# TensorE's order in a two-layer perceiver: weights turned before the next keys, norms between two halves of the values, other pauses and other places for products

## The chip, the cores and the metric

The kernel runs on one core of a Trainium2 chip. The metric is the time of one execution on the device, in microseconds (us). Its engines are TensorE (PE, with its weight loads as PEld), VectorE (DVE), ScalarE (ACT), GpSimd (POOL) and SyncE (SP), which issues most of the transfers. Each works through its own list of instructions in order and waits for the others by semaphores. All arithmetic is in float32.

## The reference, cut to what matters

`x` holds 64 batch rows of 32 tokens of 256 numbers, the context 64 rows of 257. Two layers of three steps each work on `x`; LN is a layernorm without weights.

```
x = x + cross0(ctx, LN(x))   # 16 heads x 64; keys: 257 normed context rows and the 32 queries
x = x + self0(LN(x))         # 16 heads x 16, 32 tokens, rms-normed q and k
x = x + moe(LN(x))           # 64 experts, top 8, 128 places each, and a shared expert
x = x + cross1(LN(x), ctx)   # 16 heads x 64; keys: the 257 raw context rows
x = x + self1(LN(x))         # latent heads of 32 with rotation, causal
x = x + tanh(LN(x) @ W @ A1 @ A2 + bias)
```
In `cross0` the queries and keys of each head are divided by their root mean square before they meet, so the squares of all keys must be summed before a score is complete:
```
q = (ln @ Wq); k, v = split(concat([LNg(ctx), ln]) @ Wkv)     # per head: 64 numbers
sim = (rms(q) * gq / 8) @ (rms(k) * gk).T;  out = softmax(mask(sim)) @ v;  return out @ Wout + bout
```

## The kernel before, in words

**Tiles and blocks.** The 2048 tokens are 16 tiles of 128, that is four batch rows (NB = 4) each. A batch row with its context is a block: 64 blocks s, with tile t = s // 4 and b = s % 4. `Kernel.run` calls three stages one after the other: `before` (first layer's attention and the routing, to 1568 us in the profile), `experts` (to about 1777 us) and `after` (second layer, to the end).

**What sets the order.** TensorE executes its instructions in the order in which the program writes them; the calls in the loops are that order, written by hand. The other engines' instructions are ordered by a scheduler, which also chooses, for `nc.any.tensor_copy`, whether VectorE or ScalarE copies. Products land in eight banks of TensorE's accumulator memory, which all share one rotation (`bank`): a product that needs a bank waits until the one that had it has been read.

Work that belongs to a whole tile is written as generators: `queries` ahead of a tile, `tail` and `follow` behind it. A `yield` is a pause. `slot()` lets every generator that is under way advance by one pause, tails ahead of fronts, so that pieces of a tile's work fall between the pieces of the next tile's blocks. In the first layer a block holds two `slot()` calls, or one in a tile's fourth block, where a new tail is added; in the second layer it holds three.

**First layer, one block** (`CrossFirst`, loop at the end of `before`). `load` brings the context rows (`cx`, 256 KB). `prepare` norms them (L140 on VectorE, L1160 and L1161 on GpSimd). `turn` transposes them on TensorE (L1173), and ScalarE copies them to `xT` (L1176). `keys` makes eight products with the key weights (L167, 128x289); ScalarE and VectorE copy them in turns (L1201, L1203), and ScalarE squares each half once four are there (L1206, `sq`). `norms` sums the squares on TensorE (L1218); VectorE clamps (L1226) and ScalarE takes logarithms (L1227), `nk`. `spread` brings `nk` to all rows on TensorE (L1239), and ScalarE exponentiates (L1240). `scores` are the products of queries and keys (L1258); VectorE multiplies them by the factors (L1267), adds the mask (L1268), and the softmax follows (row maximum L182 on VectorE, exponentials L184 on ScalarE, L187 to L197). `weigh` turns the weights on TensorE (L207) and copies them to `at` (L208). `values` multiplies them by the context (`weighed`, L221, eight products in two halves `kc`, and L231 for the rest of the keys) and copies both halves to `yT` (L233). The loop works on several blocks at once: in turn s it makes keys, norms and scores of block s + 2, weights and values of block s, and turns block s + 3.

**The tail of a tile** in the first layer: `heads_out` (value weights, copies `oT` L253, output weights), a pause, then `self_first`: layernorm `z`, its transposition (L149, copied to `zT` L150), the query, key and value products (`sw`, L535 to L546), transpositions (L552), scores (L573), softmax (`softmax_heads`, L267 to L271), and `attend_self` (VectorE's exponent sums and transposition L295 and L297, L310 on TensorE, `oTs` L319, output weights `swo`). In `attend_self` there is a pause before L310, and a second one only where `self.slack` is set, which is in the second layer. Then `route`: gate product, top 8, places, and the scatter of tokens to the experts' buffer (L645). The tail of the last tile but one (t == nt - 2) pauses HOLD = 5 times more ahead of `self_first`, so that it runs beside the last one's.

**Experts.** A loop over 64 experts, whose weights (L668 and L673) are fetched AHEAD = 12 experts early; pieces of the shared expert lie between them. At e == 12 `after_weights` loads and prepares the second layer's weights. Its last step is `ffn_weights`, which multiplies W, A1 and A2 of the last feed-forward into one matrix (loads `f_*`, products L167 `psA<-f_a,f_a1T` and `psA<-mid,f_wT`).

**Second layer** (`CrossSecond`, loop in `after`). Keys are never formed: `queries` makes `qk` for a tile (the key weights folded into the queries, L1308 to L1326, with the layernorm `z` of that tile ahead). In turn s come the scores of block s + 2 (L167 `psY<-xT,qk`, then maximum L1357 on VectorE, exponentials L1358 on ScalarE, scaling L1363), a `slot()`, `weigh(s)` (L1375, copies L1376), a `slot()`, `values(s)` (L167 `psA<-at,cx`, L1388), a `slot()`. Blocks 0 and 1 have two `slot()` calls more. `follow` is the tail: `heads_out`, then `self_second` (z and zT; the latent product with `wl`, L979, into the tile `lat`; L994, L995 and the rotation L988; its transposition L1003; `qTl` copied by ScalarE, L1005; the product with `wqk` and `qf`, L1011; keys turned, L1014, copied to `kTl`, L1016; scores L1026; exponentials L1036), `attend_self` and `ffn` (L1069 to L1074, and the store of the tile). The tail of the last tile but one pauses HOLD = 5 times more ahead of `self_second`. The tile `lat` has one buffer.

The start of `before` does blocks 0 and 1 in a short loop of its own (load, turn, keys, norms, spread, scores), as there is nothing to lay between.

## Time and profile before

| | |
|---|---|
| three runs | 2803.31, 2801.76 and 2800.55 us, median 2801.76 us |
| the profiled execution | 2804.67 us |
| its span, first to last instruction | 2802.8 us |
| TensorE's mean granted clock, as a share of full speed | 0.982 |
| VectorE, ScalarE, GpSimd busy | 1694.9, 1241.6 and 684.3 us |

By stage, in us (the granted clock is the mean over the stage; "DMA" is the mean busy share of the 16 transfer engines):

| stage | from | to | length | PE busy | DVE busy | ACT busy | clock | DMA |
|---|---|---|---|---|---|---|---|---|
| start, first tile | 0 | 180 | 180.0 | 143.4 | 88.6 | 78.6 | 0.93 | 0.35 |
| first layer's loop | 180 | 1525.75 | 1345.75 | 1317.1 | 859.6 | 736.2 | 1.00 | 0.08 |
| last tails | 1525.75 | 1568.5 | 42.75 | 25.1 | 24.4 | 10.0 | 0.74 | 0.59 |
| experts | 1568.5 | 1770 | 201.5 | 193.1 | 68.2 | 58.8 | 0.97 | 0.72 |
| second layer's loop | 1770 | 2700 | 930.0 | 903.6 | 603.0 | 336.7 | 1.00 | 0.20 |
| last tile and tails | 2700 | 2802.8 | 102.8 | 75.4 | 51.1 | 21.1 | 0.83 | 0.04 |

How to read the profile. A line of waits gives the engine, the tile and the line of the waiting instructions, after the arrow what released them, and then the sum of the waiting time, how often, and the longest. A line of the timeline gives the start in us, the duration of a group, the engine, line and operation, output and inputs with their shapes and the number of instructions; what stands in brackets is the time waited just before, and for whom. The busy digits of the page give tenths in 40 equal slices of the span, some 70 us each. A TensorE that is reported busy may still be slower than it could be, since the ends of its products are modelled: the distance from the start of one group to the start of the next is the surer measure.

### The profile page before, as it was taken

What the parts mean: (1) busy time and instruction counts of PE and PEld (TensorE: products, weight loads), DVE (VectorE), ACT (ScalarE), POOL (GpSimd) and SP (SyncE); (2) the same over time, 40 slices, a digit from 0 to 9 for tenths busy, and PEclk for the clock granted to TensorE, in tenths of its full rate; (3) what the DMA queues carried; (4) which work ended last, traced back from release to release, by engine and by line L of the source; (5) the groups of instructions that cost most, each with busy time, mean ns of one, the idle gap of its engine ahead of it and who ended that gap; (6) DMA issues with size and microseconds to landing.
All of it is one profiled execution on the core that took longest, in us unless ns stands there. A gap on an engine that the chain in (4) does not pass through costs nothing. (4 is left out here: it accounts for less than half of the span.)

```text
span 2802.8 us, 58905 instructions
## 1 busy us (share of the span) xinstructions
PE 2657.6 (95%) x23386; PEld 1824.5 (65%) x23386; DVE 1694.9 (60%) x4427; ACT 1241.6 (44%) x3436; POOL 684.3 (24%) x756
## 2 busy tenths in 40 slices
PE   6999999999999999999999799999999999999996
PEld 3556666666666666666666578667777777777764
DVE  5546666666666666666665433466666666666664
ACT  3455555555555555555554223333333333333331
POOL 5211333133313331243121200321212222121001
PEclk8999999999999999999999899999999999999997
DMA  8000011011000000000001677321211222222110
GB/s 271 16 14 18 31 33 31 18 31 33 29 18 27 26 22 18 20 19 16 18 7 38 233 237 243 91 67 54 58 51 50 59 52 58 56 51 55 33 35 5
DMA packets 136087, 157.03 MB, mean 56 GB/s; under 512 B 24024, under 2 KB 118979, under 8 KB 135812
## 3 DMA queue, kind: packets, MB, share of 16 engines
q1 hardware_dynamic: 114308, 119.65, 13.8%
q0 software_dynamic: 12288, 25.21, 3.4%
q10 hardware_dynamic: 9216, 8.39, 0.9%
q8 instruction: 185, 3.03, 0.4%
q14 instruction: 90, 0.74, 0.1%
HBM read 121.63 MB, written 37.75 MB: 57 GB/s over the span
## 5 line engine op out<-in xcount | busy, mean ns | idle before, releaser
L167 PE MATMUL psA<-xT,wk 128*128 128x289 f32 x2048 | 517.4, 411 | 7.9 <-ACT xT L1176 4.5
L167 PEld LDWEIGHTS psA<-xT,wk 128*128 128x128 f32 x2048 | 388.0, 191 | 134.8 <-issue 21.8
L780 POOL DMA_INDIRECT y<-oute,idx x128 | 131.5, 1028 | 643.4 <-DVE x L791 453.9
L167 PE MATMUL psA<-at,cx 128*128 128x512 f32 x512 | 235.4, 602 | 20.0 <-ACT qTl L1005 18.2
L221 PE MATMUL psY<-at,cx 128*128 128x512 f32 x512 | 239.8, 612 | 0.1
L167 PE MATMUL psY<-xT,qk 128*128 128x257 f32 x1024 | 234.3, 382 | 0.0
L167 PEld LDWEIGHTS psY<-xT,qk 128*128 128x128 f32 x1024 | 190.8, 190 | 35.0 <-issue 10.2
L1357 DVE TENSOR_REDUCE mx<-psY 128x1 f32<-128x257 f32 x256 | 105.7, 423 | 133.6 <-PE psY L167 133.5
L1358 ACT ACTIVATE sim<-psY,mx 128x257 f32<-128x257 f32 x256 | 121.6, 476 | 142.3 <-DVE mx L1357 142.2
L184 ACT ACTIVATE sim<-sim,mx 128x289 f32<-128x289 f32 x256 | 134.1, 526 | 100.0 <-DVE mx L182 100.0
L221 PEld LDWEIGHTS psY<-at,cx 128*128 128x128 f32 x512 | 93.5, 192 | 123.0 <-issue 108.8
L167 PEld LDWEIGHTS psA<-at,cx 128*128 128x128 f32 x512 | 92.9, 190 | 120.8 <-issue 76.7
L233 ACT COPY yT<-psY 128x512 f32<-128x512 f32 x127 | 68.2, 589 | 220.7 <-PE psY L231 220.7
L645 POOL DMA_INDIRECT buf<-z,fi x128 | 126.5, 988 | 148.0 <-DVE fi L642 102.2
L1160 POOL TENSOR_TENSOR cx<-cx,a_gx 128x512 f32<-128x512 f32 x64 | 81.8, 1278 | 292.1 <-DVE cx L140 290.3
L1206 ACT ACTIVATE sq<-kT 128x1156 f32<-128x1156 f32 x128 | 149.4, 1167 | 4.4 <-DVE kT L1203 2.8
L1201 ACT COPY kT<-psA 128x289 f32<-128x289 f32 x256 | 94.8, 389 | 104.2 <-PE psA L167 104.2
L1376 ACT COPY at<-psT 128x512 f32<-128x512 f32 x145 | 78.8, 595 | 123.4 <-PE psT L1375 118.3
L1218 PE MATMUL psB<-sq,c 128*32 128x289 f32 x1024 | 109.4, 419 | 19.7 <-ACT sq L1206 19.5
L1388 DVE SCALAR_TENSOR_TENSOR yT<-at,xT,psA 128x512 f32<-128x512 f32 x128 | 94.0, 735 | 56.1 <-PE psA L167 50.7
L167 PE MATMUL psY<-yT,wv 128*64 128x128 f32 x2048 | 121.6, 275 | 1.6 <-DVE yT L1388 1.4
L1177 POOL COPY xT<-lnT 128x64 f32<-128x64 f32 x64 | 15.3, 240 | 423.0 <-PE psA L167 299.3
(257 smaller groups left out, 5190.5 us busy)
## 6 DMA issues: line engine op xcount, KB each, us to landing
cx<-in_ctx SPq DMA_DIRECT2D x128, 256.0 KB
we<-in_m_ew SPq DMA_DIRECT2D x64, 384.0 KB
xT<-in_ctxT SPq DMA_DIRECT2D x64, 257.0 KB
buf<-zero SPq DMA_DIRECT2D x32, 256.0 KB
be<-buf SPq DMA_DIRECT2D x64, 128.0 KB
oute<-oe ACTq DMA_DIRECT2D x64, 128.0 KB
mu<-in_mask SPq DMA_DIRECT2D x16, 128.5 KB
x<-in_x SPq DMA_DIRECT2D x16, 128.0 KB
```

The lines of the kernel that those rows point to most:

```text
L167: self.nc.tensor.matmul(ps, lhsT=lhs[i], rhs=rhs[i], start=(i == 0), stop=(i == n - 1))
L184: nc.scalar.activation(sim[:, g, :], sim[:, g, :], AF.Exp, bias=mx[:, g : g + 1], accum_out=sm[:, g : g + 1])
L221: nc.tensor.matmul(ps[kc], lhsT=values[i][:, kc * P : (kc + 1) * P], rhs=at[i], start=(i == 0), stop=(i == n - 1 and tail is None),)
L645: d = nc.gpsimd.indirect_dma_start(out=self.buf[:, :], out_offset=bass.IndirectOffsetOnAxis(ap=fi[:, k : k + 1], axis=0), in_=z[:, 0, :], ...
L780: nc.gpsimd.indirect_dma_start(out=y, out_offset=None, in_=self.oute[:, :], in_offset=bass.IndirectOffsetOnAxis(ap=self.idx[:, t, k : k + ...
L1160: nc.gpsimd.tensor_tensor(cx, cx, self.gx.unsqueeze(1).to_broadcast([P, 2, D]), ALU.mult)
L1201: nc.scalar.copy(kT[:, p, :], ps[:, :JK])
L1206: nc.scalar.activation(sq[p // 4], kT[:, p - 3 : p + 1, :], AF.Square)
L1218: nc.tensor.matmul(ps[g * 32 : (g + 1) * 32, :JK], lhsT=k.pair[odd], rhs=sq[p // 4][:, p % 4, :], start=(odd == 0), stop=(odd == 1),)
L1357: nc.vector.tensor_reduce(mx[:, g : g + 1], ps[:, :J], AX.X, ALU.max, negate=True)
L1358: nc.scalar.activation(sim[:, g, :], ps[:, :J], AF.Exp, bias=mx[:, g : g + 1], accum_out=sm[:, g : g + 1])
L1388: nc.vector.scalar_tensor_tensor(self.yT[:, c, :, b * S : (b + 1) * S], self.at[:, 2, :].rearrange("p (h i) -> p h i", h=H), xT[:, c, J - ...
```

## The change

It moves work in TensorE's order and changes one buffer; no product is added or taken away.

- **First layer, a block.** `weigh(s)` stands ahead of `keys(s + 2)` now, not behind it. `weighed` does one half per call, and `norms(s + 2)` stands between the halves; both halves are copied to `yT` after the second.
- **`attend_self`** always has the second pause ahead of L310; before, only in the second layer.
- **The start.** The blocks 0 and 1 are written out: loads 2 to 4 come first, and `turn(1)` and `turn(2)` stand ahead of the norms of the block before.
- **HOLD** is 8 pauses in the first layer and 9 in the second, where both were 5.
- **`ffn_weights`** is called at expert 24, and no longer at expert 12 at the end of `after_weights`.
- **Second layer.** `scores(s + 2)` stands behind `weigh(s)`, between the first and the second `slot()` of a turn, where it stood ahead of both. `lat` has the two buffers of its pool.

```diff
@@ -30,7 +30,7 @@
 CAP = 128
 GT = 4
 AHEAD = 12
-HOLD = 5
+HOLD = 8, 9
 TOPK = 8
 FI = 128
 FS = 512
@@ -209,30 +209,27 @@
             k0 += n
         return [at[:n, j, :] for j, n in enumerate(sizes)]
 
-    def weighed(self, yT, b, at, values, tail=None):
+    def weighed(self, yT, b, kc, at, values, tail):
+
 
 
 
         nc = self.nc
-        ps = [self.bank("psY") for _ in range(2)]
-        n = len(at)
-        for kc in range(2):
-            for i in range(n):
-                nc.tensor.matmul(
-                    ps[kc],
-                    lhsT=values[i][:, kc * P : (kc + 1) * P],
-                    rhs=at[i],
-                    start=(i == 0),
-                    stop=(i == n - 1 and tail is None),
+        if kc == 0:
+            self.psy = [self.bank("psY") for _ in range(2)]
+        ps = self.psy
+        for i in range(len(at)):
+            nc.tensor.matmul(
+                ps[kc], lhsT=values[i][:, kc * P : (kc + 1) * P], rhs=at[i], start=(i == 0), stop=False
+            )
+        if kc == 1:
+            for c in range(2):
+                r = slice(64 * c, 64 * c + 64)
+                nc.tensor.matmul(ps[c], lhsT=tail[1][r, :], rhs=tail[0][r, :], start=False, stop=True)
+            for c in range(2):
+                nc.any.tensor_copy(
+                    yT[:, c, :, b * S : (b + 1) * S], ps[c].rearrange("p (h i) -> p h i", h=H)
                 )
-        if tail is not None:
-            for kc in range(2):
-                r = slice(64 * kc, 64 * kc + 64)
-                nc.tensor.matmul(ps[kc], lhsT=tail[1][r, :], rhs=tail[0][r, :], start=False, stop=True)
-        for kc in range(2):
-            nc.any.tensor_copy(
-                yT[:, kc, :, b * S : (b + 1) * S], ps[kc].rearrange("p (h i) -> p h i", h=H)
-            )
 
     def heads_out(self, t, yT, wv, wo, bias, split=False):
 
@@ -296,8 +293,7 @@
         eT = self.wk.tile([P, H, S], F32, name="eT", bufs=self.eb)
         nc.vector.transpose(eT.rearrange("p a b -> p (a b)"), e.rearrange("p a b -> p (a b)"))
         yield
-        if self.slack:
-            yield
+        yield
 
 
         ps = [self.bank("psY") for _ in range(NB)]
@@ -420,18 +416,22 @@
         next(first)
         next(first)
         cross.prepare(1)
-        for i in range(2):
-            cross.load(i + 2)
-            cross.turn(i)
-            cross.keys(i)
-            cross.norms(i)
-            done(first)
-            cross.spread(i)
-            cross.scores(i)
-        cross.load(4)
+        for i in range(2, 5):
+            cross.load(i)
+        cross.turn(0)
+        cross.keys(0)
+        done(first)
+        cross.turn(1)
+        cross.norms(0)
         cross.prepare(2)
+        cross.spread(0)
+        cross.scores(0)
+        cross.keys(1)
+        cross.turn(2)
+        cross.norms(1)
         cross.prepare(3)
-        cross.turn(2)
+        cross.spread(1)
+        cross.scores(1)
 
         wv = self.load(w, "wv", [P, 2, HD], a["a_wv"].rearrange("(k p) n -> p k n", p=P))
         wo = self.load(w, "wo", [P, 8, D], a["a_wo"].rearrange("(k p) n -> p k n", p=P))
@@ -488,13 +488,15 @@
                 fronts.append(cross.queries(t + 1))
             if s + 5 < n:
                 cross.load(s + 5)
+
+            cross.weigh(s)
             if s + 2 < n:
                 cross.keys(s + 2)
-            cross.weigh(s)
             slot()
+            cross.values(s, 0)
             if s + 2 < n:
                 cross.norms(s + 2)
-            cross.values(s)
+            cross.values(s, 1)
             if s + 2 < n:
                 cross.spread(s + 2)
             slot()
@@ -519,7 +521,7 @@
         yield
         if t == self.nt - 2:
 
-            for _ in range(HOLD):
+            for _ in range(HOLD[0]):
                 yield
         yield from self.self_first(t, sw, swo, sg)
         yield from self.route(t, gw)
@@ -759,6 +761,8 @@
             outer(e)
             if e == AHEAD:
                 self.after_weights()
+            if e == 2 * AHEAD:
+                self.ffnw = self.ffn_weights(self.w2)
         done(side)
 
         side, sums = shared(nt // GT - 1), self.combine(0)
@@ -803,7 +807,6 @@
         bo = self.row(w, "bo", a["b_bo"], D)
         self.weights = wq, wkT, wv, wo, bo
         self.lat = self.latent_weights(w)
-        self.ffnw = self.ffn_weights(w)
 
     def after(self, ctx):
         self.eb = self.vb = 1
@@ -838,14 +841,14 @@
             t, b = divmod(s, NB)
             if s + 3 < n:
                 cross.load(s + 3)
-            if s + 2 < n:
-                cross.scores(s + 2)
             if b == NB - 2 and t + 2 < self.nt:
                 steps.append(cross.queries(t + 2))
                 if t + 3 < self.nt:
                     steps.append(self.combine(t + 3, 3))
             slot()
             cross.weigh(s)
+            if s + 2 < n:
+                cross.scores(s + 2)
             slot()
             if s < 2:
 
@@ -863,7 +866,7 @@
         yield from self.heads_out(t, yT, wv, wo, bo)
         if t == self.nt - 2:
 
-            for _ in range(HOLD):
+            for _ in range(HOLD[1]):
                 yield
         yield from self.self_second(t, *self.lat)
         yield from self.ffn(t, *self.ffnw)
@@ -970,7 +973,7 @@
     def self_second(self, t, wl, bl, wvo, bvo, wqk, bqk, wo, bo):
         nc = self.nc
         _, zT = yield from self.normed(t)
-        lat = self.wk.tile([P, 2 * H, LAT], F32, name="lat", bufs=1)
+        lat = self.wk.tile([P, 2 * H, LAT], F32, name="lat")
         latf = lat.rearrange("p h l -> p (h l)")
         for n in range(2):
             ps = self.bank("psA")
@@ -1275,12 +1278,12 @@
         at = k.keyed(sim, [P, P, P])
         self.weights = at[:2], [cx[:, 0, :], cx[:, 1, :]], (at[2], c3)
 
-    def values(self, s):
+    def values(self, s, kc):
         k = self.k
         b = s % NB
-        if b == 0:
+        if b == 0 and kc == 0:
             self.yT = k.wkx.tile([P, 2, H, P], F32, name="yT", bufs=1)
-        k.weighed(self.yT, b, *self.weights)
+        k.weighed(self.yT, b, kc, *self.weights)
 
 
 class CrossSecond:
```

## The prediction

> **What bounds the kernel now.** I read the page's first two parts, then TensorE's waits, its timeline in each stage, and VectorE's and ScalarE's timelines beside it. The profiled execution took 2804.67 us, its span is 2802.8 and the median of the runs shown is 2801.76; the sum below is made against the profiled one, and 2.9 us come off at the end for the median.
>
> ```profile
> PE 2657.6 (95%) x23386; PEld 1824.5 (65%) x23386; DVE 1694.9 (60%) x4427; ACT 1241.6 (44%) x3436; POOL 684.3 (24%) x756
> PE   6999999999999999999999799999999999999996
> PEclk8999999999999999999999899999999999999997
> ```
> TensorE is the bound: 95% busy at a mean granted clock of 0.982. The change takes no product away, so all it can win is the 145 us of gaps, the half speed that follows them, and waits that the modelled busy time hides. TensorE's waits say where the gaps are:
>
> ```profile
> PE psB L1218 <- ACT sq L1206: 19.5, 23, 2.1
> PE psA L167 <- ACT qTl L1005: 18.2, 12, 1.7
> ...
> PE psY L310 <- DVE at L208: 14.7, 14, 1.3
> ...
> PE psA L167 <- DMA f_a<-in_f_a: 4.8, 1, 4.8
> PE psA L167 <- ACT xT L1176: 4.5, 5, 1.8
> ```
> The hidden part is read from start to start in the timeline. The norms of the keys (L1218) need 1.11 us when nothing is late (356.22 to 357.33). In the third block of a tile:
>
> ```profile
> 402.28 1.47 PE L207 MATMUL psT<-c,sim 128*128 128x128 f32 x12
> 403.59 0.60 PE L552 MATMUL psT<-c,qk 128*128 128x128 f32 x4
> 404.12 0.68 PE L1218 MATMUL psB<-sq,c 128*32 128x289 f32 x4
> 405.50 1.17 PE L1218 MATMUL psB<-sq,c 128*32 128x289 f32 x12 [0.70 <-ACT sq L1206]
> 406.60 3.70 PE L221 MATMUL psY<-at,cx 128*128 128x512 f32 x8
> ```
> From 404.12 to 406.60 is 2.48: 1.37 too much, of which the waits name 0.70. By the same reading a tile of 93.5 us loses 0.67 in its second block's norms, 1.37 in the third's, in the fourth 1.24 before L310 and 0.67 in the norms, and 0.47 at L573: 4.4 us.
>
> **1. The first layer's loop, order of a block.** After the scores come now: turned weights (L207, 1.31), keys (7.85), first half of the values (1.82), norms. Nothing is added to TensorE. What decides is how long after the scores' end the second square (L1206) is ready: VectorE's sums and row maxima, four exponentials on ScalarE, the copies of the keys. From the timelines that is about 14.0 us in the second block (scores end 649.25, square 663.26), 11.9 in the third (674.15, 686.06), 12.4 in the fourth (695.58, 707.99). The new order needs it in the third block at 0.93 (turning the queries) + 1.31 + 7.85 + 0.53 + 1.82 + 0.14 = 12.6: the 1.37 go. In the second, with 3.5 of query products and 0.8 of the tail's steps between, at about 16: the 0.67 go. In the fourth at 1.31 + 7.85 + 1.82 + 0.14 = 11.1, so 1.3 of wait stay; that block wins only 0.2, since its chain, not TensorE, sets its length. The first block wins nothing. L310 comes one pause later, behind the spreading; there it meets the wait of L573, which is 0.47. Sum 2.0 a tile, times 14 tiles with a tail beside them: **-28**. The built order puts 331 of the 384 copies `at` on ScalarE (198 now), three of 0.58 us ahead of the exponentials, while ScalarE waits for VectorE's maximum anyway (1.93 idle at 702.12): cost nothing, and up to 1.7 a block without that cover. The norms' path to the spreading (clamp 0.45, Ln 0.45, some 1.3 to 2.2 in all) keeps 3.0 of cover, from 4.8. Turning the weights needs a softmax that ended some 10 us earlier. Ends: 0 if the chain grows by 1 us; -49 if all waits but 2 x 0.47 go (3.5 x 14).
>
> **2. The start.** The first tile's blocks have no tail beside them. Keys begin at 88.91, 109.56, 134.13 and 156.66; a block without waits is 17.3 (7.91 + 1.40 + 1.11 + 3.63 + 1.06 + 0.70 + 0.53 + 1.13, with 0.93 for queries in the first), so 2.4 + 7.3 + 5.2 = 14.9 are lost. xT's copy is now covered by the weights; 1.2 of square wait a block stay: -11, and -1 for the prologue, where the norms of block 1 still wait for the same chain: **-12** (-4 to -16). Two loads `cx` (256 KB each) move ahead on SP's queue, behind the key weights, which they leave alone; the value weights behind them are first needed near 166.
>
> Here the clock matters. The windows 124 to 128 and 148 to 152 had 0.67 and 0.68 granted, after waits of 1.98 + 0.80 and 2.10.
>
> The Trainium skill ("TensorE: Matmul & The Clock Gate", "Why this matters for your kernels") has the clock fall only after gaps over about 3 us; by it these short waits would cost their length alone and the 7.3 would be some 1.5 less. The rows above show the fall after shorter gaps, so the rows count.
>
> **3. Feed-forward products at expert 24.**
> ```profile
> 1633.27 3.75 PE L167 MATMUL psA<-f_a,f_a1T 128*128 128x256 f32 x8 [4.80 <-DMA f_a<-in_f_a]
> 1636.82 2.86 PE L167 MATMUL psA<-mid,f_wT 128*128 128x256 f32 x8
> ```
> Loads issued at 1628.50 to 1629.45, because their space was the latent weights', are used at once. After a 4.80 gap the two products take 3.55 and 2.70 from start to start, 1.76 each at full clock (16 such in 3.51). In the new order SP issues them behind the same point, and TensorE has twelve experts and four shared products (about 25 us) before it needs them: 4.8 + 1.8 + 0.9 = **-7.5** (0 if they were late again). The 768 KB stand ahead of expert weights that have twelve experts of lead: nothing.
>
> **4. The second layer's start.** Scores of block 2 now stand behind the turned weights of block 0, and those behind z of tile 1.
> ```profile
> 1785.67 10.69 PE L167 MATMUL psY<-xT,qk 128*128 128x257 f32 x48
> 1800.46 0.69 PE L149 MATMUL psT<-c,z 128*128 128x128 f32 x2 [4.10 <-DVE z L140]
> ```
> The last third of the 10.69 (3.6) loses its place beside VectorE's chain. That chain loses four maxima and some 0.4 apiece, so z comes about 1.7 earlier: **+2** (0 to +5).
>
> **5. The second layer's loop.** Scores move between the turned weights and the values:
> ```profile
> 2068.21 1.47 PE L1375 MATMUL psT<-c,sim 128*128 128x128 f32 x12
> 2071.18 3.67 PE L167 MATMUL psA<-at,cx 128*128 128x512 f32 x8 [1.50 <-ACT qTl L1005]
> 2074.69 1.02 PE L167 MATMUL psB<-qTl,wqk 128*128 128x512 f32 x2
> 2075.55 0.60 PE L1014 MATMUL psT<-c,lat 128*128 128x128 f32 x4
> 2075.99 0.38 PE L149 MATMUL psT<-c,z 128*128 128x128 f32 x2
> 2076.20 3.64 PE L167 MATMUL psY<-xT,qk 128*128 128x257 f32 x16
> 2079.78 1.29 PE L1026 MATMUL psB<-kTl,qf 32*32 32x32 f32 x128
> ```
> The 1.5 a tile goes: -18.2. But the same 3.64 lay ahead of L1026, between two pauses that now follow each other. kTl's copy (0.58, some 0.8 with its signals) has only a transposition of 0.22 over it: 0.55 a tile. The same happens to zT ahead of the latent product: uncovered it costs 0.46 in the last tile (2757.62). 14 x 1.0 = +14, so **-4** (-14 if covered, +4 if z of the feed-forward, with 0.4 of slack, is late too).
>
> **6. Longer pauses.** The tail of tile 14 now runs three steps ahead of the last tile's, not six or seven. Before the experts, about 4 us of its products (z, 2.75 of sw, L552) leave the stretch ahead of 1525.75 and fill gaps behind it, where TensorE is busy 25.0 of 42.7; but VectorE's two softmax chains (6.15 from L573 to L310) then run side by side, and a step in front delays the last tile's: my walk gives +3 to the chain, 1 for two lost covers: **0** (-5 to +5). At the end, z, wl and wvo of tile 14 (5.0) move behind 2744.16, but stand between wv and wo of the last tile, 4.6 on its chain, and the second softmax adds 1 to 2: **+1** (-4 to +6). The second buffer for lat costs nothing.
>
> **Sum.** -28 - 12 - 7.5 + 2 - 4 + 0 + 1 = -48.5: 2756 for the profiled execution, **2753 us** for the median.
>
> **Rivals.**
> *The square stays late.* ScalarE's copies `at` lengthen the chain by about 1 us, 1 and 2 win nothing but 8 at the start: 2801.8 - 8 - 7.5 + 2 - 4 + 1 = 2785. For it: the fourth block is bound by that chain already. Against: ScalarE idles before the exponentials.
> *Slower.* The three copies (1.7 us) fall behind the exponentials and lengthen the chain by x: the loop then pays x in the fourth block, x - 0.7 in the third, x - 0.9 in the second. The others' 20.5 and the 28 are used up at x = 1.7 (3x - 1.6 = 3.5 a tile); at 2.2 it is 14 x 1.5 = 21 more: about 2823. Against it: in the built order the copies stand ahead of the exponentials in three blocks of four.
> *More than forecast.* The chain shortens by the `at` copies VectorE loses (0.64 each), and the fourth block's wait goes too: 1.3 x 14 = 18 more, 2735.
> *The pauses do not do what they say*: the last tails are chains of VectorE, and 6 is 0; that is in the forecast.
>
> **How the numbers follow.** Forecast 0.58, square late 0.22, more 0.14, slower 0.06. The range 2728 to 2790 takes in the first three with their ends. About 0.2% (5.6 us) can be told from no change: faster 0.91, same 0.04, slower 0.05.
>
> **What would show it.** Right: no wait of L1218 in blocks two and three, one near 1.3 in the fourth; L310's 14.7 down to some 3; no wait for f_a and 1.8 us products; qTl's 18.2 gone, with new rows for kTl near 0.5 and zT near 0.4, fourteen each; a gap near 6 before z at the second layer's start. Wrong: ScalarE's square further than 13 us from the scores' end; spreading waiting for nk; scores waiting for a bank.

## The result: slower, by as much as the forecast was faster

| | median of the runs | profiled execution | its span | granted clock |
|---|---|---|---|---|
| before | 2801.16 us | 2804.67 | 2802.8 | 0.982 |
| after | 2853.2 us | 2851.57 | 2849.7 | 0.974 |

The ratio is 1.0179, with a 95% interval of 1.0163 to 1.0195. The forecast was 2753 with a range of 2728 to 2790. The page of after:

```profile
PE 2665.8 (94%) x23386; PEld 1829.0 (64%) x23386; DVE 1658.1 (58%) x4306; ACT 1305.5 (46%) x3557; POOL 703.0 (25%) x756
PE   6999999999999999999999799899999999999995
PEclk9999999999999999999999899999999999999996
```
No product was added, and TensorE's busy time grew by 8 us where the span grew by 47. TensorE's longest waits in after, as total, count and longest:

```profile
PE psR L1242 <- ACT nk L1230: 37.9, 15, 2.8
PE psT L149 <- DVE z L140: 28.0, 9, 6.4
PE psB L1221 <- ACT sq L1209: 18.6, 19, 2.3
PE psB L1029 <- DVE qf L1014: 18.2, 13, 3.8
```
(Lines move by two to four in after: L1242 is the spreading, L1239 before; L1229 the clamp, L1226 before; L1221 the norms, L1218 before; L306 is L310 and L1029 is L1026.) The waits of L310 for the copies `at`, of the second layer for qTl, and for f_a are gone, as forecast. In their place the spreading waits for nk, which waited 1.7 us in all before.

Where the time went is seen best if the span is cut at products that have the same work ahead of them in either order: the scores of the third tile's first block, those of the last tile's, the second layer's first products of the values (psA<-at,cx), and those of its tile 14.

| stretch | before | after | change | best version (run 15) |
|---|---|---|---|---|
| start and two tiles | 226.56 | 214.65 | -11.9 | 211.63 |
| first layer, 13 tiles | 1216.56 | 1258.55 | **+42.0** | 1169.85 |
| last tile, experts, second layer's start | 367.24 | 368.46 | +1.2 | 357.52 |
| second layer, 14 tiles | 851.95 | 854.76 | +2.8 | 851.61 |
| last two tiles and tails | 140.52 | 153.31 | **+12.8** | 140.14 |

The expectations below cut the last stretch at the turned weights of tile 14, 143.85 before and 160.11 after. That mark flatters the old order: there 16 products of the scores (3.64 us) stand ahead of it, in the new one behind it, so 3.6 of those 16.3 are no loss.

A tile of the first layer went from 93.5 to 96.8 us in the mean (94.5 to 98.9). From keys to keys, its four blocks took 20.5, 21.6, 29.6 and 21.9 before, and in the mean 19.2, 21.0, 30.1 and 26.5 after. The fourth loses 4.6 and the third 0.5; the other two gain. (Blocks are counted here by the keys that are made, the first being those of b = 0. The prediction counts by the turn, two blocks behind: its third, fourth, first and second block are the first to fourth here.) TensorE's timeline of one such fourth block in after:

```profile
655.41 7.97 PE L167 MATMUL psA<-xT,wk 128*128 128x289 f32 x32
663.22 0.33 PE L167 MATMUL psA<-sel,c 128*128 128x64 f32 x2
663.39 0.39 PE L167 MATMUL psA<-count,c 128*128 128x64 f32 x2
...
665.65 1.21 PE L1221 MATMUL psB<-sq,c 128*32 128x289 f32 x16
666.79 1.99 PE L222 MATMUL psY<-at,cx 128*128 128x512 f32 x4
668.71 1.13 PE L228 MATMUL psY<-at,c 64*128 64x512 f32 x4
672.61 1.34 PE L1242 MATMUL psR<-nk,c 32*128 32x289 f32 x8 [2.77 <-ACT nk L1230]
673.88 3.92 PE L167 MATMUL psA<-sw,zT 128*128 128x512 f32 x8
```
The two `sel` and `count` lines are the tail's products for the places of its tokens. They stand behind the keys now. Before, one pause earlier, they stood ahead of them:

```profile
742.78 0.43 PE L167 MATMUL psA<-sel,c 128*128 128x64 f32 x2
743.05 0.39 PE L167 MATMUL psA<-count,c 128*128 128x64 f32 x2
...
746.76 7.97 PE L167 MATMUL psA<-xT,wk 128*128 128x289 f32 x32
...
756.19 1.85 PE L1218 MATMUL psB<-sq,c 128*32 128x289 f32 x16
```
In after the norms follow, the second half of the values, and a hole of 2.77 us. The eight products of sw behind it take 3.92 where they take 2.85 in before: for 3.41 us from 672.67 the granted clock was 0.50. VectorE's timeline in the same stretch of after tells why nk is late:

```profile
664.29 2.58 DVE L140 TENSOR_SCALAR cx<-cx,mv,rs 128x256 f32<-128x256 f32 x2
667.39 0.97 DVE L631 TENSOR_TENSOR val<-val,kept 128x64 f32<-128x64 f32 x1
668.65 1.04 DVE L636 SCALAR_TENSOR_TENSOR junk<-val,v,pr 128x64 f32<-128x64 f32 x1
...
671.41 0.28 DVE L636 SCALAR_TENSOR_TENSOR junk<-val,v,pr 128x64 f32<-128x64 f32 x1
...
671.62 0.46 DVE L1229 TENSOR_SCALAR nk<-psB 128x289 f32<-128x289 f32 x1
```
The norms ended at 666.86; the clamp began 4.76 later, after seven of the eight accumulations (L636) and what belongs to them. In before it began 0.22 after the norms (758.04 to 758.26), with this chain already done, by 753.66:

```profile
753.36 0.28 DVE L634 SCALAR_TENSOR_TENSOR junk<-val,v,pr 128x64 f32<-128x64 f32 x1
...
758.26 0.45 DVE L1226 TENSOR_SCALAR nk<-psB 128x289 f32<-128x289 f32 x1
```
So the theory to test was: **the extra pause in `attend_self` moved not only L310 but everything behind it in the tail, and put VectorE's place chain (L627 to L644) ahead of the clamp.** (A first-layer block holds three `slot()` calls, and a tile's fourth turn two, not two and one as said ahead of the prediction: a tile has eleven pauses.) The rival: the new order of a block leaves too little cover between norms and spreading whatever the pauses are.

### The profile page after: what moved, and what is told of

The parts are those of the page before. It is cut to its first block, busy times and chain, and to the rows that moved or that the text cites. A ratio compares the mean times of both kernels' runs of the same rounds, so it can differ in the third digit from the quotient of the medians.

```text
span 2849.7 us, 58999 instructions
## 1 busy us (share of the span) xinstructions
PE 2665.8 (94%) x23386; PEld 1829.0 (64%) x23386; DVE 1658.1 (58%) x4306; ACT 1305.5 (46%) x3557; POOL 703.0 (25%) x756
## 3 DMA queue, kind: packets, MB, share of 16 engines
q8 instruction: 185, 3.03, 0.4%
## 5 line engine op out<-in xcount | busy, mean ns | idle before, releaser
L222 PE MATMUL psY<-at,cx 128*128 128x512 f32 x512 | 248.6, 609 | 0.0
L222 PEld LDWEIGHTS psY<-at,cx 128*128 128x128 f32 x512 | 88.6, 190 | 95.6 <-issue 92.9
L647 POOL DMA_INDIRECT buf<-z,fi x128 | 128.6, 1005 | 55.2 <-issue 36.1
L1206 DVE COPY kT<-psA 128x289 f32<-128x289 f32 x256 | 109.5, 450 | 17.3 <-PE psA L167 16.5
L167 PEld LDWEIGHTS psY<-yT,wv 128*64 128x64 f32 x2048 | 113.2, 137 | 9.7 <-issue 4.8
L1180 POOL COPY xT<-lnT 128x64 f32<-128x64 f32 x64 | 21.3, 332 | 394.1 <-PE psA L167 280.9
L167 PE MATMUL psY<-wo,oT 128*128 128x256 f32 x512 | 117.6, 383 | 0.0
L1270 DVE TENSOR_TENSOR sim<-psB,sim 128x289 f32<-128x289 f32 x256 | 101.3, 448 | 27.7 <-PE psB L1261 27.6
```

What stands on the lines that cost most here:

```text
L167: self.nc.tensor.matmul(ps, lhsT=lhs[i], rhs=rhs[i], start=(i == 0), stop=(i == n - 1))
L222: nc.tensor.matmul(ps[kc], lhsT=values[i][:, kc * P : (kc + 1) * P], rhs=at[i], start=(i == 0), stop=False)
L647: d = nc.gpsimd.indirect_dma_start(out=self.buf[:, :], out_offset=bass.IndirectOffsetOnAxis(ap=fi[:, k : k + 1], axis=0), in_=z[:, 0, :], ...
L1206: nc.vector.tensor_copy(kT[:, p, :], ps[:, :JK])
L1270: nc.vector.tensor_tensor(sim[:, g, :], ps[i][:, :JK], sim[:, g, :], ALU.mult)
```

## The experiments

Runs 1 to 4, 5 to 8, 9 to 12 and 13 to 15 were each on one chip, and not on the same. On two of these, and on the result's, before takes 2801 to 2802 us; on two (runs 1 to 8) it takes 2821. So a run is compared with before on its own chip, and stretches between chips of one kind. Runs 4 to 6, 9, 10, 13 and 14 are single executions.

**1. One pause ahead of L306 in the first layer.**
```diff
-        yield
+        if self.slack:
+            yield
```


> The changed kernel with one pause ahead of L306 in the first layer again (the second only in the second layer). Theory A, place chain: the extra pause puts the 17 VectorE instructions of a tile's places (L627 to L644) ahead of the clamp of the fourth block's norms (L1229), so the spreading (L1242) waits 2.8 us and TensorE runs 1.1 to 2.5 us slower behind it. Without the pause they stand ahead of the keys' copies, as before: the waits of L1242 for nk (37.9 us) go, the fourth block falls from 26.1 to 27.5 down to 22 or less, a tile takes 91 to 93 us (now 96.2 to 97.6; 93.5 before), and the kernel about 2853 - 14 x 4.6 = 2789 us (2780 to 2800). Theory B, cover: the new order of a block leaves half of the values as cover between the norms and the spreading, which is too little with or without the pause: L1242 still waits over 25 us in all, a tile stays above 95 us, the kernel above 2835 us.

Measured: 2789.15 us on a chip where before takes 2820.61, ratio 0.9886 (0.9869 to 0.9902). The 13 tiles took 1198.2 us, 87.5 less than in the next run, which has both pauses on the same chip. Theory B, above 2835, is out. That the expected 2789 was met is luck: it was counted down from 2853, and on a chip of this kind after takes 2894 (run 6), so the pause cost more here. Not as expected: L1242 still waited 20.6 us in all; see "a second kind of chip" below. Run 12 shows that wait gone on the first kind.

**2. HOLD at 5 and 5.**
```diff
-HOLD = 8, 9
+HOLD = 5, 5
```


> The changed kernel with HOLD at 5 pauses in both layers again. Theory A: the last 160.1 us (from the start of tile 14's blocks in the second layer; 143.9 before) are long because the tails of tiles 14 and 15 run as chains side by side behind the last block, each step of the one in front of the other; with 5 pauses they fall back to about 145 us, and the end of the first layer (372.8 us between the last tile's first keys and the second layer's first turned weights) changes by less than 3: about 2853 - 15 = 2838 us. Theory B: the stretch is long because the scores now stand behind the turned weights; then it stays at about 160 us and the kernel at 2853.

The last stretch took 147.15 us, not 160.1 (140.3, not 153.3, by the table's mark): theory A. The total, 2882.42 (ratio 1.0215, 1.0198 to 1.0232), was not the 2838 expected, since this chip loses more in the loop (1285.7 us against 1258.6 for the same code).

**3. Pause behind the norms.**
```diff
-            slot()
             cross.values(s, 0)
             if s + 2 < n:
                 cross.norms(s + 2)
+            slot()
             cross.values(s, 1)
```


> The changed kernel with the pause between keys and values moved behind the norms: first half of the values, norms, pause, second half. Both pauses ahead of L306 stay. Theory A, place chain: the places' VectorE work now stands behind the clamp in program order, so the wait of L1242 goes with the extra pause in place: a tile at 91 to 94 us, the kernel at 2785 to 2805. The square may be waited for a little more, 1 to 2 us a tile, since the pause's products no longer lie ahead of the norms. Theory B, cover: the wait of L1242 stays, a tile above 95, the kernel above 2835.

The clamp followed the norms' end by 0.05 us in all 14 tiles and the wait for nk was gone: so far theory A. But the kernel took 2892.61 us (1.024, 1.022 to 1.0259), a miss for both. In its place TensorE waits at L1138 and L207 for nothing that the profile names, 17.8 and 17.7 us in all; in run 2, on the same chip and with the pause where it was, these were 14.4 and 3.4. What the edit does on a chip of the first kind was not run. TensorE's timeline behind the fourth block's scores:

```profile
684.24 0.33 PE L1138 MATMUL psT<-c,q 128*128 128x128 f32 x1
685.32 0.60 PE L1138 MATMUL psT<-c,q 128*128 128x128 f32 x4 [0.75 <-issue]
686.78 0.53 PE L1138 MATMUL psT<-c,q 128*128 128x128 f32 x3 [0.86 <-issue]
```

**4. The pause alone, added to before.** (The diff of run 1 reversed, on before.)


> The kernel before with nothing changed but the second pause ahead of L310. Theory A: the wait of L310 for VectorE's copies (14.7 us) goes, and the place chain now stands ahead of the clamp here too; but all eight products of the values and the rest (4.8 us) lie between norms and spreading, and only the 8 or 9 first of the chain stand ahead of the clamp, so at most 1 us of wait a tile comes: 2787 to 2805 us. Theory B (the pause is harmless): 2787 us and no wait of L1239 for nk.

2946.23 us where before takes 2820.61: a large miss, in the direction of the theory, though not by the clamp: it is 3.9 behind the norms in the fourth block, but no spreading waits there. The pause is worse still in the old order: a tile's second block takes 24.2 us (21.6) and its fourth 28.6 (21.9 to 23.4 in before on such a chip), and the norms wait for the square 53 times (53.7 us). I had looked at the clamp alone, though the pause moves oTs, z, gate and places, each into another block's chain.

**5 and 6. Before and after again, on one chip.**


> The kernel before, unchanged, with a trace from the chip of this call. Theory A (chips differ): in the runs so far the kernel before took 2801 us on one chip and 2821 on another. If this call's chip is like the first, the trace is that of before: a tile of 93.5 us, the clamp of the fourth block's norms 0.2 us behind the norms' end, the total near 2801. If it is like the second, 1.4 us a tile are lost while GpSimd issues the scatter (L645), in TensorE's issue or in the clamp, and the total is near 2821: 14 x 1.4 = 20. Theory B (the loss came from the changed order alone): tiles of 93.5 us on any chip, and the 20 us lie elsewhere.

> The changed kernel, unchanged, on the chip of this call. On a chip like the first: tiles of 96.2 to 97.6 us and about 2853 us. On one like the second: tiles of 98 to 99 us, as in the run with HOLD 5, and some 13 us more at the end than that run: 2880 to 2895 us. In both the clamp of the fourth block starts 4.7 us behind the norms' end, since that is the places' chain on VectorE.

2821.64 and 2894.32 us, the second kind of chip. The last stretch was 143.8 and 159.9 (140.4 and 153.0 by the table's mark): the end's loss is the same on both kinds. The loop was 1228.6 and 1295.5.

**7. One pause, HOLD 8 and 5.**
```diff
-HOLD = 8, 9
+HOLD = 8, 5
```


> The changed kernel with one pause ahead of L306 in the first layer, and HOLD at 8 in the first and 5 in the second layer. Theory A: the two losses add up, so against the run with one pause alone it wins the end's 13 us: the stretch from tile 14's first turned weights in the second layer to the end is about 147 us, not 160, and the ratio to before about 0.9886 - 13/2820 = 0.984. Theory B (the end is long because of the scores' new place): the stretch stays at 160 and the ratio at 0.9886.

2778.56 us, ratio 0.9848 (0.9832 to 0.9864), the last stretch 147.3 (140.5 by the table's mark): theory A, within 0.001.

**8. And the second layer's scores back ahead of the pause.**
```diff
+            if s + 2 < n:
+                cross.scores(s + 2)
             if b == NB - 2 and t + 2 < self.nt:
...
             cross.weigh(s)
-            if s + 2 < n:
-                cross.scores(s + 2)
```


> The kernel of the run before this one, with the second layer's scores back ahead of the pause, where the kernel before has them. Theory A: the scores' new place trades one wait for another, since 1.5 us for qTl in each tile became 1.2 us for qf, and in some tiles 1 to 2 us more at a lower clock; with the old place the second layer's regular stretch of 14 tiles takes 858.0 us as before, 2 less than after, and its last stretch 143.9, 3 less than with the scores moved: 3 to 6 us faster than the run before. Theory B, as forecast (-4 for the move): 4 us slower.

2770.89 us, ratio 0.9826 (0.981 to 0.9842), 7.7 less than run 7. The second layer's 14 tiles took 851.6 (857.9 in run 7): theory A, and more than its 3 to 6. The last stretch went from 147.3 to 143.3 by the expectation's mark, but from 140.5 to 140.0 by the table's, so the scores' place costs the end 0.5. HOLD 9 is the rest of the end's +12.8: 12.6 from run 6 to 7, 9.9 from run 1 to 2 (both pairs also differ in the first layer).

**9 and 10. After and before without GpSimd's scatter.** (The eight `indirect_dma_start` of L647 taken out.)


> The changed kernel without GpSimd's scatter (L647, eight a tile): the tokens are not brought to the experts, which work on the cleared buffer; all else stays. Theory A (two separate losses): the place chain on VectorE is still there, so the clamp of the fourth block starts 3.5 to 4.7 us behind the norms' end and L1242 still waits in each tile; but what the second and third chip lost on top (tiles of 98 to 99 us where the first had 96.2 to 97.6) goes, on any chip: tiles of 95.5 to 97.5 us, no issue waits at L1138, about 2840 to 2855 us in all. Theory B (the scatter itself is what moved into the way): the clamp starts within 1 us of the norms' end, tiles fall below 93 us, the kernel below 2810.

> The kernel before without GpSimd's scatter (L645), the same part left out as in the run before this one. Theory A: on the second and third chip TensorE's completions were seen by the other engines only when the scatter had landed (the clamp 3.6 to 5.1 us behind the norms' end, 0.2 on the first). Without a scatter the clamp follows within 0.3 us on any chip, the tile takes 93.5 us or a little less, and the kernel 2795 to 2803 us where before takes 2821 on the same chip. Theory B (another cause on those chips): the clamp stays late and the kernel at 2821.

2843.51 and 2801.79 us; before took 2801.53 on this chip. After's loop was 1254.8 (1258.6 with the scatter): its loss is there without any scatter, as theory A has it. Of the second kind of chip these two runs say nothing, since theirs is of the first.

**11. The fourth block's pause ahead of the spreading.**
```diff
+            if b == 1:
+                slot()
             if s + 2 < n:
                 cross.spread(s + 2)
-            slot()
+            if b != 1:
+                slot()
```


> The kernel of the run with one pause, HOLD 8 and 5 and the scores back (2770.9 us, 0.9826 of before, on the third chip), with the second pause of a tile's fourth block moved ahead of the spreading: 2.85 us of the tail's products (sw) then lie between norms and spreading, beside the half of the values. Theory A (the spreading waits for nk 1.5 to 2.1 us because the clamp is held while the scatter lands): the wait of L1243 (21.6 us in all) goes, the fourth block takes 21.9 us in every tile, 15 to 22 us less on a chip like the second and third (ratio 0.975 to 0.978), 0 to 5 less on one like the first. Rival: the factors of the scores come 2.85 us later and the softmax with them, so the next block's square is waited for instead: no gain.

2751.23 us, 0.9819 (0.9803 to 0.9835), loop 1176.4. Against run 12 on the same chip the fourth block takes 21.70, not 21.22: on this chip, where nk is in time, the edit costs 0.5 a tile. There is no gain, as the rival has it, but not for its reason: the wait for the square is 7.6 us in all in both runs. What it would do on the second kind stays open.

**12. What is left: order of a block, start, lat.**
```diff
-HOLD = 8, 9
+HOLD = 5, 5
...
         self.lat = self.latent_weights(w)
+        self.ffnw = self.ffn_weights(w)
...
-            if e == 2 * AHEAD:
-                self.ffnw = self.ffn_weights(self.w2)
```
together with the diffs of runs 1 and 8.


> The changed kernel with one pause, HOLD 5 and 5, the scores back and the feed-forward products back at expert 12: what is left of the change is the order of a block in the first layer, the start, and the second buffer of lat. Against the run with HOLD 8 and 5 and the scores back (0.9826 of before): the feed-forward products wait for f_a again and run at half clock, 3.3 to 5 us in the experts' stretch (about 208 us from the first shared product to the last expert, 203 with the later place), and the last tails before the experts change by under 5 us. Together 3 to 9 us slower: ratio 0.984 to 0.986.

2741.61 us, ratio 0.9788 (0.9772 to 0.9804): better than expected. The loop took 1169.9 us, a tile 89.98, with 19.2, 19.9, 29.7 and 21.2 in its blocks, and TensorE's waits in 13 tiles add up to 2.5 us, all of them at L573 (0.2 a tile). The clamp stands 0.07 us behind the norms, and the spreading waits for nothing. The experts' stretch was 208.1, as expected with the products early. From the last turned weights of the first layer to the first shared product it took 52.4; run 11, with HOLD 8, took 58.0. So HOLD 8 costs 5.6, where the pause is single; run 7, which has no moved pause, also took 58.0, on the other kind of chip.

**13. The place chain shortened.**
```diff
-        for k in range(TOPK):
-            nc.vector.scalar_tensor_tensor(
-                junk, val, v8[:, k : k + 1], pr, ALU.is_equal, ALU.mult, accum_out=self.w8[:, t, k : k + 1]
-            )
+        nc.vector.tensor_copy(self.w8[:, t, :], top)
```


> The changed kernel, both pauses and HOLD 8 and 9, without the eight accumulations that bring the routing weights into the order of the places (L636, 8 a tile): the eight best weights are copied as they come, so the experts' outputs are weighted wrongly. Theory A (the length of VectorE's chain): 8 x 0.28 to 0.36 = 2.3 to 2.9 us less stand ahead of the clamp, which starts about 2 us behind the norms' end, not 4.7; the half of the values covers 3.0, so the wait of L1242 falls from 2.8 to under 1 a tile, the clock stays up behind it, a tile takes 91 to 94 us (96.2 to 97.6), and the kernel 2780 to 2805 us where after takes 2853, on a chip like the first. Theory B (GpSimd's arithmetic on cx, or the scatter, holds VectorE anyway): the clamp stays 4 us or more late, tiles above 95.

2811.19 us, just above the expected 2780 to 2805; before took 2801.94. The clamp stood 3.16 behind the norms (I had said 2), and L1242 waited 1.17:

```profile
656.44 1.13 PE L228 MATMUL psY<-at,c 64*128 64x512 f32 x4
658.74 0.77 PE L1238 MATMUL psR<-nk,c 32*128 32x289 f32 x8 [1.17 <-ACT nk L1226]
659.44 2.85 PE L167 MATMUL psA<-sw,zT 128*128 128x512 f32 x8
```
The tile took 93.2 us and the loop 1215.3, 43 less than after. Half of the pause's loss in the loop is thus the length of these accumulations: 1.6 of wait a tile, and the granted clock, which has no low stretch in this loop (sw 2.85 behind 1.17) and twelve in after's.

**14. Before without the scatter, once more.**


> The kernel before without GpSimd's scatter, once more (the tokens are not brought to the experts). On a chip where before takes about 2821 us: theory A (the scatter's landing holds TensorE's completions) 2795 to 2805 us, the clamp within 0.3 us of the norms' end; theory B 2815 to 2825. On a chip where before takes about 2801 us both give 2802, as in the first such run.

2799.74 us, on a chip of the first kind again. Not settled.

**15. Run 12 with the feed-forward products at expert 24.**


> The kernel of the order_only run (0.9788 of before) with the feed-forward products at expert 24 again. The experts' stretch went from 208.1 to 205.0 us with them there, so 3 us less: 2738.5 us on a chip like the first, ratio about 0.978. On a chip like the second or third the fourth block's spreading waits 1.5 to 2 us a tile, some 20 us more in both kernels: ratio about 0.981.

**2734.45 us, ratio 0.976 (0.9744 to 0.9777): the fastest version, 67 us under before.** Expected were 3 us less than run 12; it is 7.2. The experts' stretch fell to 200.5, by 7.6. Its fourth block has no wait at all:

```profile
723.37 1.18 PE L1222 MATMUL psB<-sq,c 128*32 128x289 f32 x16
724.48 1.98 PE L222 MATMUL psY<-at,cx 128*128 128x512 f32 x4
726.39 1.13 PE L228 MATMUL psY<-at,c 64*128 64x512 f32 x4
727.45 0.77 PE L1243 MATMUL psR<-nk,c 32*128 32x289 f32 x8
728.15 2.85 PE L167 MATMUL psA<-sw,zT 128*128 128x512 f32 x8
```

## Why the prediction was wrong, step by step

| step | forecast | in after | by itself |
|---|---|---|---|
| 1 loop of the first layer | -28 | +42.0 | order -46.6 (13 tiles, run 12); pause +88.6 (after against run 12) |
| 2 start | -12 | -11.9 | -15.0 (run 12); 9 to 15 over all runs |
| 3 products at expert 24 | -7.5 | -3.3 in the experts' stretch | -7.6 (runs 12 and 15); less with HOLD 8 |
| 4 second layer's start | +2 | -0.1 | |
| 5 second layer's loop | -4 | +4.6 | +6.4 for the whole layer up to tile 14 (runs 7 and 8) |
| 6 HOLD, before the experts | 0 | +2 | +5.6 with one pause (runs 11 and 12) |
| 6 HOLD and scores, at the end | +1 | +12.8 | HOLD 9 +9.9 to +12.6, scores +0.5 |

**1 failed, and with it the sign.** The step read: "L310 comes one pause later, behind the spreading; there it meets the wait of L573, which is 0.47", and "the norms' path to the spreading (clamp 0.45, Ln 0.45, some 1.3 to 2.2 in all) keeps 3.0 of cover". The pause was costed for the instruction it stands in front of. Everything behind it in the same generator moves one pause as well, on VectorE too, and the last part of that, the places, came to lie between keys and norms. The path of 1.3 to 2.2 became 5.75, of which 4.76 are ahead of the clamp, and it had 2.98 of products over it. The list of signs had this ("spreading waiting for nk"), but the sum gave it no price.

The failure lies in one block. In us a tile, the prediction's third block changed by -1.27 (worked out: 1.37 won), its fourth by -0.56 (0.2 won), its first by +0.47 (nothing), and its second by +4.62 (0.67 won). Nor was the pause needed for what it was to do: in run 12, which has one, L310 waits for no copy either.

Of the 6.8 us a tile that the pause costs (88.6 / 13), 2.75 are the wait for nk, and 2.2, as an estimate, the clock: twelve stretches at half speed in the loop, 58.0 us long, where before and run 12 have none. 0.8 are squares waited for (10.3 in the 13 tiles, none in run 12); this is the wait that the prediction left in its fourth block, as 1.3. The other 1.0 was not taken apart.

The order of the block itself, forecast with the pause at -28 and an end of -49 "if all waits but 2 x 0.47 go", won 47. By the prediction's blocks run 12 has -1.29 in the third, -0.65 in the second and +0.09 in the first, as worked out, but -1.71 in the fourth: with one pause the 1.29 of L310 stay ahead of the norms there, and no square is waited for. (The 0.67, 1.37 and 0.2 of the step add up to 2.24 a tile, not 2.0.) ScalarE took the copies `at` without harm in run 12 (188 of the first layer's 192, where before has 53), so the rival "the square stays late" and the rival "slower" by those copies are both refuted. A slower kernel came, but by a mechanism that no rival of mine held.

**2 came near, in part by luck.** Between the keys at 88.91 and those at 156.66, for which -11 was worked out, 67.75 us became 59.45 (59.50 in run 12): 8.3 less. The rest came ahead of them, where -1 was given, and from three turns of tile 1. Nor is the sum firm: in five traces with the old start this stretch took 222.6 to 226.6, and in six with the new one and one pause 211.3 to 213.6. (A block without waits adds up to 17.47, not 17.3, which takes 0.5 off the 14.9.)

**3 was right in its mechanism, and in runs 12 and 15 to 0.1.** The two products in after:

```profile
1695.89 1.89 PE L167 MATMUL psA<-f_a,f_a1T 128*128 128x256 f32 x8
1697.62 2.19 PE L167 MATMUL psA<-mid,f_wT 128*128 128x256 f32 x8
```
They follow without a gap, 1.73 from start to start, where 1.76 was given for full speed. The size depends on what else stands there: in the runs that keep the scatter, the stretch up to the last expert takes 186.8 to 187.5 with the early place, 179.9 and 180.4 with the late one and HOLD 5, and 181.5 to 184.4 with HOLD 8. In after 3.8 of it went back in other waits: the transposition of the expert's rows waited 6.6 us for their transfer `be`, 2.8 before.

**4 did not come.** From the first scores to tile 1's first products of the values it took 78.14 before and 78.08 after. Over all runs it is 76.8 to 78.4 with the old order and 77.6 to 79.0 with the new, too close to tell from nothing. z came 1.17 earlier (13.62 behind the first scores, not 14.79), where 1.7 was forecast.

**5: the exchange was seen, its price not.** qTl's 18.2 went, as said, and a wait under the two joined pauses came. It is not kTl that is late by 0.55, though, but qf (VectorE, L1014) by 1.20, and zT by 0.24. A regular tile is 61.36 against 61.54: a gain of 0.18, where I said 0.29. What turned it into a loss are five tiles with 1.0 to 1.8 more, each with one hole of 0.88 to 1.62 without a releaser; one of them reads:

```profile
2105.22 1.28 PE L1029 MATMUL psB<-kTl,qf 32*32 32x32 f32 x128 [1.20 <-DVE qf L1014]
2106.43 0.94 PE L167 MATMUL psA<-zT,wq 128*128 128x128 f32 x6
2108.99 3.06 PE L167 MATMUL psA<-zT,wq 128*128 128x128 f32 x26 [1.62 <-issue]
```
A hole in which TensorE waits for no other engine; the last section says what stands beside it.

**6 at the end was mis-sized**: +1, with an upper end of +6, against 12.8. I let three products change places and added 1 to 2 for the second softmax. In the runs the tails of tiles 14 and 15 go through their chains side by side behind the last block. The timeline of after's end:

```profile
2803.84 1.49 PE L1029 MATMUL psB<-kTl,qf 32*32 32x32 f32 x123 [3.78 <-DVE qf L1014]
2807.51 0.32 PE L1029 MATMUL psB<-kTl,qf 32*32 32x32 f32 x5 [2.19 <-issue]
...
2819.41 0.36 PE L1029 MATMUL psB<-kTl,qf 32*32 32x32 f32 x15 [2.03 <-issue]
...
2825.61 0.66 PE L149 MATMUL psT<-c,z 128*128 128x128 f32 x2 [3.83 <-DVE z L140]
```
From tile 14's first turned weights on, TensorE's waits add up to 29.0 us, 19.4 before: those for z are 12.4 (3.9 before), and the two holes at L1029 are 4.2 (none before). The granted clock is at half for 45.8 us there, 36.3 before. VectorE's list holds both tails in turns, but it idles between the pieces (3.39 ahead of 2819.81), so these are waits for both chains' length more than for VectorE's time.

## What to carry to other kernels

A pause put into a generator moves everything that the generator still has to do, on all engines: list what is behind it, and see in which block's critical chain each piece lands. Where an engine's list is in order, cover between a product and its use must outlast not the chain of the result alone but whatever the scheduler has put ahead of it there. And test edits that share a change one by one: here a gain of 47 us, one of 9 to 15 and one of 3 to 8 were hidden under losses of 89 and 13. Marks for such a comparison must have the same products ahead of them in both orders.

## What the runs showed of the hardware that was not expected

**Gaps of under 3 us were followed by half the clock.** In after's loop the 13 waits of 2.75 to 2.77 were followed by low stretches of 3.4 or 6.8 us in twelve tiles, where sw took 3.8 to 5.3 us, and by none in one, where it took 2.85. With the same waits it was eleven of 13 in run 2 and eight of 13 in run 6; behind 2.0 to 2.1 it was five of eight in run 1, and behind 1.17 none of 13 in run 13. The Trainium skill ("TensorE: Matmul & The Clock Gate", "What's actually happening") speaks of a free-running window of 3413 ns, which agrees with these lengths; its rule of no gaps over some 3 us ("Why this matters for your kernels") is too generous here.

**VectorE's instructions stretched beside GpSimd's arithmetic.** In after's block above, two normalisations of cx took 2.58 us where four take 1.50 elsewhere (run 1), L631 0.97 and the first L636 1.04 where they take 0.21 and 0.28 in before. Each ended within 0.15 us of the end of a GpSimd product on cx (L1163 and L1164: 666.72, 668.27, 669.62). L631 and one L636 are that long in 13 of after's 16 tiles and in none of before's. That GpSimd holds them is read from these times; no run took its products away.

**Holes behind dense small products.** The holes without a releaser in after's second layer shown above stand behind 128 products of 32x32 that take 1.28 us, or among them. Queue q8, which carries 3.03 MB of instructions in 185 packets of 16 KB, loaded one during each: landed at 2107.55, 2806.00 and 2818.11, and TensorE went on at 2108.99, 2807.51 and 2819.41, 1.3 to 1.5 us after. In the old order 3.64 us of large products stood ahead of L1026 and no such hole appeared. That the load is the cause is argued from these times; no run took it away. The Trainium skill ("Runtime: NRT & Kernel Launch", "Instruction fetch mechanics") has the refill in 16 KiB blocks, as seen, and its cost mostly hidden, which fits most of the 185 packets, but not these three.

**A second kind of chip.** On two of the chips before takes 20 us more. Its clamp starts 3.6 to 5.1 us behind the norms of the fourth block in the loop's 13 tiles (run 5; 0.22 on the first kind), with VectorE idle; VectorE's and then TensorE's row in before's trace there:

```profile
763.26 0.46 DVE L1226 TENSOR_SCALAR nk<-psB 128x289 f32<-128x289 f32 x1 [4.79 <-PE psY L231]
764.25 0.77 PE L1239 MATMUL psR<-nk,c 32*128 32x289 f32 x8 [1.39 <-ACT nk L1227]
```
In run 1 the trace's semaphore events show four completions of TensorE together at 645.43 to 645.58, the norms' among them though these had ended at 641.44, and the last scatter's landings at 645.37 to 645.52; the delays come in steps near 1.4 us, and a scatter is issued every 1.28. It looks as if completions wait for the scatter there. Neither run without a scatter met such a chip, so this stays open.
